# A hybrid attention block: the first batches' statistics, norm and values moved to ScalarE and GpSimd, and the end of attention in another order

## The chip, the cores and the metric

The kernel runs on one core of a Trainium2 chip. The core has TensorE (matmuls, written PE in the profile, with its weight loads as PEld), VectorE (DVE), ScalarE (ACT), GpSimd (POOL) and SyncE (SP), which issues most of the transfers. The metric is the device time of one execution in microseconds; the median over runs is compared.

## The reference

Input is `x`, 8 batches of 512 tokens with 256 channels, all in float32. Four blocks are added to it one after the other, each on the layer norm of `x`: an attention, a routed feed-forward, a gated linear attention with a SwiGLU, and the same routed feed-forward again. The change lies in the first block, except for one edit in the last.

```python
def _L0_attn_a_ref(x, Wq, bq, Wk, bk, Wv, bv, Wo, bo):      # H = 16 heads of 16 channels
    U = max(1, min(L, int(FACTOR * L)))                     # 307 of 512 queries
    q = _split_heads(x @ Wq + bq)
    k = _split_heads(x @ Wk + bk)
    v = _split_heads(x @ Wv + bv)
    scores = jnp.einsum('bhqd,bhkd->bhqk', q, k) * scale
    sparsity = scores.max(axis=-1) - scores.mean(axis=-1)
    _, top_idx = jax.lax.top_k(sparsity, U)
    ...                                                     # the chosen queries alone:
    attn = jax.nn.softmax(scores_sel, axis=-1)
    out_sel = jnp.einsum('bhuk,bhkd->bhud', attn, v)
    out = jnp.zeros_like(q).at[bi, hi, top_idx].set(out_sel)
    return out @ Wo + bo

x = x + _L0_attn_a_ref(_layernorm(x, axis=-1), ...)
x = x + _L0_ffn_ref(_layernorm(x, axis=-1), ...)
x = x + _L0_attn_b_ref(_layernorm(x, axis=-1), ...)
x = x + _L0_ffn_ref(_layernorm(x, axis=-1), ...)
```

A query that is not among the 307 of its head gives zero, so the kernel computes the attention of all queries and multiplies each result by one over its sum, or by zero.

## The kernel before

`xres` holds all of `x` in SBUF as 128 tokens x 8 batches x 4 token tiles x 256 channels. The attention works batch by batch. `front(b, pick, alone)` prepares a batch: the norm `xn` (L337 to L346), its transposes `xnT` (L357) and a centred copy `xcT` (L366 on ScalarE or L369 on VectorE), then the projections `q_ps` and `k_ps` (L384), evacuated as `qs` and `ks`, and the values `v_ps` (L423), written with their bias into `va` (L432). Queries and keys exist twice, for even and odd heads (`e`), so that four heads lie in four groups of 32 rows of TensorE.

One loop over `n` drives it. There are 128 steps of (batch, half `m`, parity `e`, token tile `k`). In each, `max_one` makes four score tiles (L487) and VectorE takes the maximum of each row into `mx` (L490). Sixteen steps later (`LAG = 16`) `exp_one` makes the transposed scores of the same heads (L498), ScalarE takes the exponential (L502), and `weigh` multiplies by the values into `av` (L507). So for the first 16 steps there are maxima alone. This is called the fill below. Here the rest of `front(0)` and all of `front(1)` are laid between the steps, piece by piece:

```python
            LAG = 16
            LEAD = 14
            ...
            first = front(0, lambda name: next(both)(name), True)
            for _ in range(6):
                next(first)
            pieces = itertools.chain(first, front(1, lambda name: next(alone)(name), True))
```

The fronts of batches 2 to 7 are laid between later steps with `alone` false. The maxima's negatives go through a transpose and small DMAs on SP into a spare row of the queries (`place_maxima`, L459) and into `neg`, one row for each batch and head.

The order of instructions on each engine is worked out by the framework, which plans with its own costs, starts from the order of the text, and keeps what depends on each other. Where the text would be planned too early, a tiny copy on GpSimd from a maximum of a given step (`maximum_of(n)`) is written into the target first, so that the instruction has to wait for it. `batch_stats` (L262) makes mean and variance of a batch on VectorE (L275, L276), the root on ScalarE (L279), its reciprocal on VectorE (L280) and a shift (L283). It is called for batch 0 ahead of the loop, for batch 1 at n = 1 (held to `xcT` of batch 0), for batch 2 at n = 5, and for batches 3 and 4 to 7 in `later_stats`, spread over the loop.

When all maxima are there, `top_queries` finds on VectorE, for the 128 rows of `work`, which queries are dropped (L536, L539). `take` (L517 to L525) copies a finished `av`, sends the rows that hold the sums of the exponentials to `den` by DMA on ScalarE's queue, and puts the rest into `outC`. `weights_of` forms `nrm` = 1/`den` where a query is chosen and 0 elsewhere (L137, L138). `weigh_outputs` spreads rows of `nrm` over channels with a small matmul (L150, a strip of 32 rows of TensorE holds two batches) and multiplies `outC` (L153). `out_unit(tail, k, b)` projects two batches' token tile `k` with `wo_a` (L163), copies on ScalarE and adds into `xres` on GpSimd. `out_projection` does the rest later with an addition on VectorE (L849, L853), and `route(0)` begins the routed feed-forward with statistics of `xres`. In the last block `down` (L955) adds the second product of a pair of batches into `xres` (L969) and sends the result out (L972).

Of the kernel before, what the change touches and what calls it, by code (L numbers as in the profile page):

```python
# [10 lines left out]
F32 = mybir.dt.float32  # L11
U8 = mybir.dt.uint8
AF = mybir.ActivationFunctionType
ALU = mybir.AluOpType
# [3 lines left out]
P = 128  # L18
# [20 lines left out]
def block_kernel(ctx: ExitStack, tc: tile.TileContext, t: dict, out: bass.AP):  # L39
# [62 lines left out]
    with ExitStack() as outer:  # L102
# [14 lines left out]

        outC = [
# [3 lines left out]
        den = a_out.tile([P, L], F32, name="den")  # L122
        neg = a_out.tile([P, L], F32, name="neg")
        mx = a_out.tile([P, NB, NC2, 2, 4 * 4], F32, name="mx")
# [5 lines left out]
        def weights_of(batches, late, late_form):  # L130


            rows = slice(16 * batches[0], 16 * batches[-1] + 16)
# [3 lines left out]
            nc.vector.reciprocal(rden[rows, :], den[rows, :])  # L137
# [5 lines left out]
        def weigh_outputs(batches):  # L143
            picks = itertools.cycle((bank, bank_m))
            for u in range(2):
                for m in range(NC2):
                    for b in batches[u::2]:
                        strip = bass.ts(b // 2, 32)
                        ps = next(picks)(f"nrm_ps{b}")
                        nc.tensor.matmul(  # L150
                            ps, spread[strip, u, m, :], nrm[strip, :], start=True, stop=True
                        )
                        nc.vector.tensor_tensor(  # L153
                            outC[b][:, m, :], outC[b][:, m, :], ps, ALU.mult
                        )
# [16 lines left out]
        with ExitStack() as inner:  # L172
# [48 lines left out]
            own = a1.tile([P, 2], F32, name="own")  # L221
            one = a1.tile([P, 2], F32, name="one")
            kept = a1.tile([P, 2], F32, name="kept")
# [34 lines left out]
            clear_values(0)  # L258

            ln = {}  # L260

            def batch_stats(batches, late=None, late_shift=None):  # L262


# [3 lines left out]
                st = a2.tile([P, n, 6], F32, tag="ln_st", name="ln_st")  # L268
                mv = a1.tile([P, n, 2], F32, tag=f"ln_mv{key}", name="ln_mv")
                rs = a1.tile([P, n], F32, tag=f"ln_rs{key}", name="ln_rs")  # L270
                sh = a1.tile([P, n], F32, tag=f"ln_sh{key}", name="ln_sh")
                for i in range(n):
                    if late is not None:
                        nc.gpsimd.tensor_copy(st[0:1, i, 0:1], late())
                    nc.vector.bn_stats(st[:, i, :], xres[:, batches[i // 4], i % 4, :])  # L275
                    nc.vector.bn_aggr(mv[:, i, :], st[:, i, :])  # L276
                    if i < n - 1:
                        yield
# [1082 lines left out]
```

## Time and profile before

| | |
|---|---|
| median of 3 runs | 1623.8 us (1623.19, 1623.8, 1629.82) |
| the profiled execution's own time | 1629.82 us |
| its span, first to last instruction | 1628.1 us |
| granted TensorE clock over the span | 0.992 |
| TensorE, VectorE, ScalarE, GpSimd busy | 98%, 60%, 42%, 21% of the span |
| the 512 maxima (L490) | 328.0 us of VectorE, 683 ns each |
| the 512 exponentials (L502) | 276.4 us of ScalarE, 597 ns each |
| first score matmul, first exponential | at 16.23 us, at 66.61 us |
| last `av` matmul ends, routed hidden matmuls begin to run together | at about 579.6 us, at 627.8 us |

A row of the profile names line, engine, operation, what is written and read, and busy time. TensorE's busy share is no measure of how full it is, since matmuls overlap and their ends are modelled. What counts for a change is the stage in which it lies and which engine is short there: the fill (up to about 66 us), the loop (to 535), the choice of queries and the last exponentials (to 580), the end of attention (to 628), and the long rest of feed-forwards and linear attention.

### The profile page before, as it was taken

What the parts mean: (1) busy time and instruction counts of PE and PEld (TensorE: products, weight loads), DVE (VectorE), ACT (ScalarE), POOL (GpSimd) and SP (SyncE); (2) the same over time, 40 slices, a digit from 0 to 9 for tenths busy, and PEclk for the clock granted to TensorE, in tenths of its full rate; (3) what the DMA queues carried; (4) which work ended last, traced back from release to release, by engine and by line L of the source; (5) the groups of instructions that cost most, each with busy time, mean ns of one, the idle gap of its engine ahead of it and who ended that gap; (6) DMA issues with size and microseconds to landing.
All of it is one profiled execution on the core that took longest, in us unless ns stands there. A gap on an engine that the chain in (4) does not pass through costs nothing.

```text
span 1628.1 us, 19814 instructions
## 1 busy us (share of the span) xinstructions
PE 1590.0 (98%) x7444; PEld 814.7 (50%) x7444; DVE 971.6 (60%) x2007; ACT 676.8 (42%) x1215; POOL 348.5 (21%) x403
## 2 busy tenths in 40 slices
PE   7999999999999999999989999999999999999999
PEld 3323323233233256655564566545655655766666
DVE  7868777676777875447753566367265633344342
ACT  3366656565655834352346124522631452121010
POOL 2111111010010043115332343145234320000000
PEclk9999999999999999999999999999999999999999
DMA  3100000000000032100000001000000010011100
GB/s 108 42 3 2 2 2 3 3 3 2 2 3 4 2 110 86 27 14 13 0 0 1 1 0 27 1 0 1 1 0 1 1 27 0 21 33 39 40 27 26
DMA packets 24951, 27.62 MB, mean 17 GB/s; under 512 B 6872, under 2 KB 21400, under 8 KB 24856
## 3 DMA queue, kind: packets, MB, share of 16 engines
q1 hardware_dynamic: 24040, 25.31, 5.4%
q8 instruction: 58, 0.95, 0.2%
q10 hardware_dynamic: 816, 1.05, 0.2%
q14 instruction: 37, 0.30, 0.1%
HBM read 21.24 MB, written 4.33 MB: 16 GB/s over the span
## 4 chain that ended last, share of the span: by engine, by line
PE 78%; DVE 12%; ACT 4%; POOL 3%; issue 2%; DMA 1%; SPq 0%; ACTq 0%; POOLq 0%; DVEq 0%
PE y_ps L964 16%; PE h_ps L984 10%; PE s L487 9%; PE s L498 9%; PE av L507 8%; PE swi_ps L1011 7%; PE proj_ps L1097 7%; DVE pr L1130 2%; DVE pr L1120 2%; PE q_ps L384 2%; PE gla_y L1222 2%; PE k_ps L384 2%; PE v_ps L423 2%; POOL o L1147 2%; DVE w L1122 1%
## 5 line engine op out<-in xcount | busy, mean ns | idle before, releaser
L490 DVE TENSOR_REDUCE mx<-s 128x1 f32<-128x512 f32 x512 | 328.0, 683 | 118.8 <-PE s L498 63.5
L502 ACT ACTIVATE e<-s 128x512 f32<-128x512 f32 x512 | 276.4, 597 | 185.2 <-PE s L498 106.8
L487 PE MATMUL s<-k,q 32*128 32x512 f32 x1024 | 301.8, 644 | 3.7 <-ACT k L414 3.2
L498 PE MATMUL s<-q,k 32*128 32x512 f32 x1024 | 297.8, 642 | 0.1
L964 PE MATMUL y_ps<-w,h 128*128 128x256 f32 x1024 | 232.5, 383 | 2.8 <-DVE h L993 2.8
L984 PE MATMUL h_ps<-xnT,w 128*128 128x512 f32 x512 | 230.1, 598 | 4.1 <-ACT h L992 4.1
L964 PEld LDWEIGHTS y_ps<-w,h 128*128 128x128 f32 x1024 | 194.0, 192 | 39.9 <-issue 10.1
L984 PEld LDWEIGHTS h_ps<-xnT,w 128*128 128x128 f32 x512 | 95.3, 191 | 112.5 <-issue 106.0
L507 PE MATMUL av<-e,va 128*32 128x512 f32 (+1 forms) x1240 | 144.4, 530 | 4.6 <-ACT e L502 3.2
L993 DVE TENSOR_TENSOR h<-h,mk 128x512 f32<-128x512 f32 x128 | 97.9, 779 | 79.7 <-ACT h L992 61.6
L487 PEld LDWEIGHTS s<-k,q 32*128 32x128 f32 x1024 | 93.9, 184 | 96.3 <-DVE mx L490 52.2
L992 ACT ACTIVATE h<-h_ps,b 128x512 f32<-128x512 f32 x96 | 65.4, 685 | 176.1 <-PE h_ps L984 176.1
L498 PEld LDWEIGHTS s<-q,k 32*128 32x128 f32 x1024 | 91.1, 183 | 75.6 <-ACT e L502 50.3
L969 DVE TENSOR_TENSOR xres<-xres,y_ps 128x512 f32<-128x512 f32 x48 | 32.8, 683 | 160.7 <-PE y_ps L964 123.5
L1011 PE MATMUL swi_ps<-zT,w_gate 128*128 128x512 f32 x256 | 122.6, 599 | 4.8 <-DVE h L1020 4.6
L1011 PE MATMUL swi_ps<-zT,w_up 128*128 128x512 f32 x256 | 121.4, 594 | 0.0
L964 PE MATMUL y_ps<-w_down,h 128*128 128x256 f32 x512 | 116.9, 380 | 0.0
L1097 PE MATMUL proj_ps<-q_w,rT 128*128 128x512 f32 x256 | 116.1, 594 | 0.3 <-ACT al L1080 0.3
L964 PEld LDWEIGHTS y_ps<-w_down,h 128*128 128x128 f32 x512 | 95.6, 190 | 19.5 <-issue 8.0
L1017 ACT ACTIVATE h<-swi_ps 128x512 f32<-128x512 f32 x64 | 38.2, 596 | 155.5 <-PE swi_ps L1011 155.3
L1147 POOL TENSOR_TENSOR o<-o,pr 128x512 f32<-128x512 f32 (+2 forms) x56 | 81.1, 1449 | 58.6 <-DVE pr L1130 56.6
L507 PEld LDWEIGHTS av<-e,va 128*32 128x32 f32 x1240 | 25.5, 108 | 123.6 <-issue 102.4
(203 smaller groups left out, 1722.1 us busy)
## 6 DMA issues: line engine op xcount, KB each, us to landing
mk<-md SPq DMA_DIRECT2D x32, 256.0 KB
out<-xres SPq DMA_DIRECT2D x16, 256.0 KB
xres<-in_L_attn_a_x SPq DMA_DIRECT2D x7, 512.0 KB
q<-negT SPq DMA_DIRECT2D x128, 2.0 KB
neg<-negT SPq DMA_DIRECT2D x128, 2.0 KB
w<-in_f_w1T SPq DMA_DIRECT2D x1, 1024.0 KB
w<-in_f_w2T SPq DMA_DIRECT2D x1, 1024.0 KB
w_gate<-in_b_w_gateT SPq DMA_DIRECT2D x1, 1024.0 KB
```

What stands on the lines that cost most here:

```text
L487: nc.tensor.matmul(s, qs[e][rows, m, bass.ts(k, P)], ks[e][rows, m, :], start=True, stop=True)
L490: nc.vector.tensor_reduce(mx[:, b, m, e, r : r + 1], s, AX.X, ALU.max)
L498: nc.tensor.matmul(s, ks[e][rows, m, bass.ts(kt, P)], qs[e][rows, m, :], start=True, stop=True)
L502: nc.scalar.activation(ex, s, AF.Exp, scale=1.0 / DH**0.5)
L507: nc.tensor.matmul(av[32 * j : 32 * j + 32, queries], va[:, 8 * kt + 4 * m + j, e, :], es[j][:, queries], start=(kt == 0), stop=(kt == 3 a ...
L964: nc.tensor.matmul(y[0][:, bass.ts(i, D)], h[f][:, bass.ts(2 * u + i, P)], w[:, f, :], start=(f == 0), stop=(f == NF - 1),)
L984: nc.tensor.matmul(ps, w1[:, c, bass.ts(f, P)], xT[g][:, c, :], start=(c == 0), stop=(c == NC2 - 1),)
L992: nc.scalar.activation(hf, ps, AF.Relu, bias=b1[:, f : f + 1])
L993: nc.vector.tensor_tensor(hf, hf, mk[g][:, f, :], ALU.mult)
L1011: nc.tensor.matmul(ps, w[:, c, bass.ts(f, P)], zT[g][:, c, :], start=(c == 0), stop=(c == NC2 - 1),)
L1097: nc.tensor.matmul(ps, rT[b // G4][:, c, bass.ts(b % G4, P)], q_w[:, c, m], start=(c == 0), stop=(c == NC2 - 1),)
L1147: nc.gpsimd.tensor_tensor(dst, dst, src, ALU.add)
```

## The change

- `early_stats` replaces `batch_stats` for batches 1 and 2. It sums `x` and the squares of `x` less its mean by accumulating activations on ScalarE, takes the root there, and leaves a reciprocal to VectorE and the shift to GpSimd. Both are held to the maximum of the step before. After batch 2's root an exponential of one column is issued.
- The norm of batches 1 and 2 is made on GpSimd as a multiply and add; batch 1's was on ScalarE, batch 2's on VectorE. The centred copy of batch 2 goes from VectorE to ScalarE.
- The values of batches 0 and 1 are copied out of PSUM by ScalarE and get their bias on GpSimd.
- The roots of batches 3 and 4 to 7 are made by three rounds of Newton's iteration on GpSimd from a first guess in integer arithmetic on VectorE.
- A batch's rows in `den`, `neg` and `nrm` are placed by `row_of`, so that neighbouring batches lie in different strips. `den` becomes two tiles, for batches 0 to 5 and 6 to 7, both filled with ones. `mx` holds four batches in turn.
- Outputs are weighed pair by pair, with output units between the pairs.
- In the last pair of the last tile each batch is added and sent out by itself.

```diff
+        def row_of(b, m, e):
+            return 32 * (b % 4) + 16 * (b // 4) + 8 * e + 4 * m
...
-        mx = a_out.tile([P, NB, NC2, 2, 4 * 4], F32, name="mx")
+        mx = a_out.tile([P, 4, NC2, 2, 4 * 4], F32, name="mx")
...
+        picks = itertools.cycle((bank, bank_m))
+        def weigh_outputs(b):
+            for m in range(NC2):
+                for c in (b, b + 1):
+                    strip = bass.ts(c % 4, 32)
+                    ps = next(picks)(f"nrm_ps{c}")
+                    nc.tensor.matmul(
+                        ps, spread[strip, c // 4, m, :], nrm[strip, :], start=True, stop=True
+                    )
+                    nc.vector.tensor_tensor(
+                        outC[c][:, m, :], outC[c][:, m, :], ps, ALU.mult
+                    )
...
+            for i in range(2):
+                nc.gpsimd.memset(den[i], 1.0)
...
+            def early_stats(b, late):
+                sm = a1.tile([P, 3, 4], F32, tag=f"ln_sm{b}", name="ln_sm")
+                sums, less, squares = (sm[:, i, :] for i in range(3))
...
+                own = a2.tile([P, L], F32, tag="e", name="ln_x", bufs=10)[:, 0:D]
+                for i in range(4):
+                    nc.gpsimd.tensor_copy(sums[0:1, i : i + 1], late)
+                    nc.scalar.activation(
+                        own, xres[:, b, i, :], AF.Identity, accum_out=sums[:, i : i + 1]
+                    )
+                nc.gpsimd.tensor_scalar(less, sums, -1.0 / D, None, ALU.mult)
+                for i in range(4):
+                    nc.scalar.activation(
+                        own, xres[:, b, i, :], AF.Square, bias=less[:, i : i + 1],
+                        accum_out=squares[:, i : i + 1],
+                    )
+                nc.scalar.activation(rs, squares, AF.Sqrt, bias=eps, scale=1.0 / D)
+                if b == 2:
+                    nc.scalar.activation(root, rs[:, 0:1], AF.Exp)
+                nc.vector.reciprocal(rs, rs)
+                nc.gpsimd.tensor_tensor(sh, less, rs, ALU.mult)
...
+            def one_by_root(rs, var, n):
...
+                nc.gpsimd.tensor_scalar(v, var, LN_EPS, None, ALU.add)
+                nc.vector.tensor_scalar(
+                    rs.bitcast(I32), v.bitcast(I32), -0.5, float(0x5F3759DF), ALU.mult, ALU.add
+                )
+                for _ in range(3):
+                    nc.gpsimd.tensor_tensor(u, v, rs, ALU.mult)
+                    nc.gpsimd.tensor_tensor(u, u, rs, ALU.mult)
+                    nc.gpsimd.tensor_scalar(u, u, -0.5, 1.5, ALU.mult, ALU.add)
+                    nc.gpsimd.tensor_tensor(rs, rs, u, ALU.mult)
...
-                    if alone and b > 0:
-                        nc.scalar.activation(
-                            xn[:, k, :], xres[:, b, k, :], AF.Identity, bias=sh, scale=rs
+                    if sh is not None:
+                        nc.gpsimd.tensor_scalar(
+                            xn[:, k, :], xres[:, b, k, :], rs, sh, ALU.mult, ALU.add
                         )
...
-                    if alone and b > 0:
+                    if b in (1, 2):
                         nc.scalar.mul(mean, xsum[:, c : c + 1], -1.0 / L)
                         nc.scalar.activation(xcT[:, c, :], ps, AF.Identity, bias=mean)
...
+                        if alone:
+                            nc.scalar.copy(home, v)
+                            nc.gpsimd.tensor_tensor(home, home, bias, ALU.add)
+                        else:
+                            nc.vector.tensor_tensor(home, v, bias, ALU.add)
...
-                    for _ in batch_stats(batches, lambda: maximum_of(n - 1)):
+                    for _ in batch_stats(batches, lambda: maximum_of(n - 1), True):
...
-            near = {
-                1: batch_stats([1], lambda: fronts[0][3][0:1, 1, 0:1], maximum_of(0)),
-                5: batch_stats([2], lambda: maximum_of(n - 1)),
-            }
...
-                    for _ in near.get(n, ()):
-                        pass
+                    if n in (1, 5):
+                        early_stats(1 + n // 5, maximum_of(n - 1))
...
-            weigh_outputs(range(NB - 2))
-            last = outC[NB - 3][0:1, 1, 0:1]
-            weights_of(range(NB - 2, NB), last, last)
+            for b in (0, 2):
+                weigh_outputs(b)
             for k in range(2):
-                for b in range(0, NB - 2, 2):
+                out_unit(tail, k, 0)
+            weigh_outputs(4)
+            last = outC[5][0:1, 1, 0:1]
+            weights_of(slice(P // 2, P), 1, last, last)
+            for b in (2, 4):
+                for k in range(2):
                     out_unit(tail, k, b)
-            weigh_outputs(range(NB - 2, NB))
+            weigh_outputs(6)
...
-            if i == 1 and half == 1:
+            if last and k == 3 and b == NB - 2:
+                if half == 1:
+                    x = xres[:, b + i, k, :]
+                    nc.vector.tensor_tensor(x, x, y[0][:, bass.ts(i, D)], ALU.add)
+                    nc.sync.dma_start(out=out_v[:, b + i, k, :], in_=x)
+            elif i == 1 and half == 1:
                 nc.vector.tensor_tensor(tokens(k, b), tokens(k, b), pairs(y[0]), ALU.add)
```

## The prediction

> **What bounds the kernel now.** I read the page's busy shares first, then the windows, then the chain of waits and the timeline of the stages that the diff touches.
>
> ```profile
> PE 1590.0 (98%) x7444; PEld 814.7 (50%) x7444; DVE 971.6 (60%) x2007; ACT 676.8 (42%) x1215; POOL 348.5 (21%) x403
> ```
>
> TensorE fills the span, so VectorE's 60% says little by itself. The windows show that the first stage is of another kind (columns: stretch, length, then PE, PEld, DVE, ACT, POOL busy, granted clock, DMA share, GB/s):
>
> ```profile
> 20.00:40.00 20.00, 19.93 (x87) 9.19 (x85) 18.80 (x42) 6.45 (x14) 4.91 (x12) 0.99 0.24 76
> 40.00:60.00 20.00, 19.56 (x81) 7.90 (x80) 19.10 (x37) 5.93 (x9) 7.49 (x6) 1.00 0.20 61
> ...
> 200.00:240.00 40.00, 40.00 (x254) 12.14 (x251) 29.80 (x52) 23.95 (x48) 5.17 (x4) 1.00 0.01 2
> ```
>
> From 20 to 60 us VectorE is busy 37.9 of 40 us and ScalarE 12.4, GpSimd 12.4. From 200 on VectorE has a quarter to spare and TensorE none. So work taken off VectorE pays only in the fill, the first 16 steps, which make maxima and no exponentials. The chain of waits says what starts the fill and what paces it (start, us, what):
>
> ```profile
> 7.38 5.96 DMA xres<-in_L_attn_a_x
> ...
> 14.96 0.23 DVE ln_mv L276 x2
> 15.19 0.03 issue
> 15.22 0.03 ACT ln_rs L279
> 15.24 0.18 issue
> 15.42 0.77 ACT k L414
> 16.19 0.04 issue
> 16.23 1.43 PE s L487 x8
> ...
> 53.02 4.86 DVE mx L490 x8
> 57.87 0.66 DVE va L432 x2
> 58.54 2.42 DVE mx L490 x4
> 60.96 0.66 DVE va L432 x2
> 61.62 2.39 DVE mx L490 x4
> ```
>
> The first score matmul waits for k, and k stands on ScalarE behind a root that waits for the statistics of batch 1, whose data land at 13.3. Later the chain is maxima (4 in 2.4 us) with values between them. In the loop one wait of TensorE touches the change (total us, times, longest), beside one row of ScalarE's timeline:
>
> ```profile
> PE av L507 <- ACT e L502: 3.2, 2, 1.8
> ```
>
> ```profile
> 108.85 1.28 ACT L279 ACT_TABLE_LOAD   x1
> ```
>
> **The change part by part.** *Start.* Batch 1's statistics leave the front of the queues: they now wait for the first maximum. The projection for k ends at 13.0 (timeline: `k_ps` at 11.14 for 1.89), its first evacuation takes 0.77, so scores start at 13.8, not 16.23: minus 2.4 us. ScalarE pays later: 8 passes of 128x256 at 0.52 (four `xn` in 2.08) plus 0.19 for each accumulator read, a root of 0.30 and two hand-overs to GpSimd of some 0.3 are 6.6 us. This runs from about 16 to 23 and delays batch 0's second query evacuation (22.84 before) by little. Then GpSimd normalizes: four at 0.615 (row L1229, 128x256) are 2.5 us, done by 26 to 28. The transposes that need it stood at 34.4, and at 29 to 30 with the other gains. TensorE's queue is in order, so a later `xn` would stop the score matmuls behind it; there are about 2 us to spare. GpSimd's own queue holds the clearing of `va` (1.8) behind it, which batch 1's values need only after 50.
>
> *Fill.* What leaves VectorE after 17.6: eight value additions, 3.0 us; batch 2's statistics, four pairs at a pitch of 0.34 plus 0.09, 1.7; its `xn`, 1.3; its shift, 0.1; its first centred copy with the mean, 0.9. Together 7.0, less 0.2 for the reciprocal of batch 1 that now falls here: 6.8. ScalarE gains 6.6 for batch 2 (in its gap between 27.3 and 35.6), eight value copies at about 0.4, 3.2, and 1.8 for the centred copies (0.69 and 0.20 twice); it loses `xn`, 2.1. Its 26 us before 66 become 42, still under the 50 or so there. GpSimd gains five normalizations' worth, 2 x 2.5, and eight additions at 0.77 (row L1089) to 0.90 (L1161), 6 to 7: its 18 become 30. No DMA is moved past another on SP; only the loads' triggers come earlier with the maxima.
>
> Here a rule speaks against the change. The GpSimd row for 128x256 is 0.615 and VectorE's is 0.394; the Trainium skill, "GPSIMD Engine Reference", section 4.1 Engine selection, says that ordinary elementwise work belongs on VectorE, GpSimd being about twice as slow with two inputs, and section 1 that its SBUF interface is shared with VectorE. By the rule the moved work costs more and might slow VectorE too. The trace has a test: from 51.5 to 58.5 GpSimd adds without pause, and eight maxima take 4.88, 0.61 each, as in 61.54 with GpSimd idle (2.47 for four). So I charge no contention; by the rule 64 maxima slowed by a tenth would take 4 us back.
>
> Without the 6.8 VectorE needs 64 x 0.61 = 39.0 plus 1.7 of small work. TensorE needs as much: 16 x 1.07 for scores, 7.9 for the rest of batch 0's front (four projections at 1.0, values 3.9), 13.1 for batch 1's, 1.2 of transposes: 39.3. Two engines that hand over through seven banks will not both run full, so I take 5.5 of the 6.8 (bounds 2 and 6.8).
>
> *Entry to the loop.* Batch 2's second centred copy, 0.9, leaves VectorE, and the exponential's table is loaded early: before, the load stood from 65.32 to 66.60 with the first scores ready. Against this ScalarE makes the two centred copies amid its first exponentials. Minus 1.5 (bounds plus 1 and minus 3).
>
> *Loop.* The roots of batch 3 and of batches 4 to 7 take no table. The trace shows two switches there and back, 1.28 per load with nothing after it, 5.1 us of ScalarE; TensorE lost 1.4 and 1.8. The Trainium skill, "ScalarE: Activation LUTs", section What ACT_TABLE_LOAD costs, puts a switch at 2.66 with its drain: 10.6, and TensorE would gain 8. The activation at 110.14 follows the load of 108.85 at once, so the trace decides: minus 3.2. Newton's 13 GpSimd operations, at 0.19 each by the smallest rows, are 2.5 us twice on an engine 13% busy; VectorE's one is 0.2. What waits behind them is `outC`, used at 580. I take minus 3.0.
>
> *End of attention.* Rows are laid out so that neighbours b and b+1 have different strips, and outputs 0 to 5 are weighed pair by pair. Before, twelve products (0.62 each from 581.47) stood in an order by which output units started at 585.85 and ran from 587.65; pair 0 is now ready after four, 583.95. The units then fill TensorE while the other products run: minus 2 at the first unit. Later 8 units at 1.78 (9.33 for 42 matmuls) and three weighing groups end near 600, where out_projection started at 605.94. The second reciprocal (3.35) comes no earlier than before, and it feeds batches 6 and 7: their products can't end before 598. Between 0 and minus 6 I take minus 4. The fill of `den` with ones is two memsets of a quarter of `va`'s 1.80 each, before 7 us, when GpSimd waits for weights anyway.
>
> *Last tile.* The last addition is 0.4 instead of 0.69 and the last transfer half as large; but the first addition reads half of a bank whose other half TensorE is about to write, which the trace shows nowhere. If that serializes, TensorE stands for 0.5. Bounds minus 0.7 and plus 0.6; I take 0.
>
> The sum is 2.4 + 5.5 + 1.5 + 3.0 + 4.0 = 16.4. The profiled execution took 1629.8 (span 1628.1), so it would be 1613.4. That execution is 6 us above the median and holds stretches at half clock (68 to 75 us at 0.50), of which I count nothing as gained. From the median, 1623.8, the forecast is 1607.4.
>
> **Rivals.**
> *TensorE takes over the fill.* Its 39.3 is as long as VectorE's new total, its queue is in order, and 7 steps from 44.5 to 62.0 already ran at 2.5 us. If the pace stays near 2.9 instead of 3.1 per step, the fill yields 3; with 1.5 at the end of attention and the start and loop as above the sum is 9.9: 1614. For it: score loads wait both for maxima and for issue. Against it: TensorE waits on VectorE in half of the early steps.
>
> *ScalarE becomes late in the fill.* Its queue carries statistics, values and centred copies between the evacuations that free banks. If every evacuation is late by 0.5, 16 of them take 8 back; the start and the loop remain, in part: 4 us, 1620. Against it: gaps of 6 to 8 us stand in its row before.
>
> *The loop's rhythm breaks: slower.* The engines' orders are planned anew. Between 80 and 530 us I read 204 half-steps whose eight score records stand together: 152 took 1.1 us, 26 took 1.3, 14 took 1.4, where banks came free in pairs. Each break costs 0.25 with no other engine to absorb it. `mx` now has four batches, so maxima also wait for transposes, and starts shift. With 100 more broken half-steps, 25 us, all is lost and 8 more: 1632. It decides against the change from 66 on. Against it: those transposes are 64 steps old, and nothing of the loop's bank use is edited.
>
> **How the numbers follow.** A measurement of this kernel can tell about 0.5%, 8 us, from no change: faster means below 1615.7. The forecast has a chance of 0.62, with its own range of 1601 to 1614. TensorE in the fill has 0.20, of which three parts in four lie below 1615.7. ScalarE late has 0.10, and the broken rhythm 0.08, most of it slower. That makes faster 0.77, same 0.16, slower 0.07. The range of 1600 to 1620 leaves out the slow case, half of the ScalarE case and a twentieth below.
>
> **What would show it.** Right: first scores near 13.8; VectorE between 15 and 56 nearly all maxima at 0.61; the first exponential scores near 56 instead of 64.5; no table load between 70 and 580 and no 1.4 us stop of `av`; the first output unit some 2 us after the first weighing, and the first routed hidden matmuls 16 us earlier. Wrong: transposes of batch 1 waiting for `xn`, scores waiting for ScalarE's value copies, more half-steps of 1.3 us, or the gain at 80 us gone by 540.

## The result, and the profile after

| | us | runs |
|---|---|---|
| before, on the same chip | 1627.4 | 6, from 1623.2 to 1629.9 |
| after | 1637.3 | 6, from 1634.3 to 1639.1 |
| ratio | 1.0063, 95% interval 1.0043 to 1.0082 | |

The changed kernel is slower, by 0.6%. The forecast was 1607.4. The kernel before was timed again in five later sets of 14 to 44 runs, with medians of 1627.7 to 1629.1, so the 1623.8 from which the forecast was set out was low by about 4.

The profiled execution of the changed kernel took 1634.33 us (span 1632.5). Its first row, the busy shares, says little:

```profile
PE 1584.1 (97%) x7444; PEld 810.5 (50%) x7444; DVE 958.7 (59%) x1971; ACT 681.8 (42%) x1250; POOL 366.1 (22%) x450
```

VectorE has lost 13 us of work, ScalarE and GpSimd have gained 5 and 18, all as intended. The windows say where the time went (columns: stretch, length, then PE, PEld, DVE, ACT, POOL busy, granted clock, DMA share, GB/s):

```profile
20.00:40.00 20.00, 16.70 (x71) 7.08 (x70) 12.30 (x24) 11.59 (x34) 8.74 (x20) 0.91 0.18 57
40.00:60.00 20.00, 17.96 (x70) 6.49 (x71) 16.15 (x30) 9.33 (x19) 8.73 (x11) 0.91 0.23 61
...
100.00:120.00 20.00, 13.97 (x81) 4.64 (x82) 9.81 (x20) 8.59 (x16) 7.04 (x17) 0.86 0.01 3
...
200.00:220.00 20.00, 16.09 (x97) 4.79 (x94) 11.85 (x23) 7.74 (x15) 4.82 (x10) 0.83 0.00 1
```

From 20 to 60 VectorE is busy 28.5 of 40 us instead of 37.9, but TensorE too has lost: 34.7 instead of 39.5, and its clock is down. An engine that was relieved and then stands idle was not the only bound, or now waits for something. And in two stretches of the loop, where TensorE had nothing to spare, it stands for 6.0 and 3.9 us. TensorE's list of waits (engine, line, releaser: total us, times, longest) gives them names:

```profile
PE s L539 <- DVE mx L542: 11.4, 4, 6.0
PE xnT_ps L405 <- DVE xn L392: 6.7, 2, 6.5
PE swi_ps L1069 <- DVE h L1078: 5.1, 7, 1.4
PE q_ps L432 <- ACT xcT L414: 4.3, 1, 4.3
```

The second is at the very start and the third in the SwiGLU of the third block, and the kernel before has both. The first and the fourth are new. What `mx` waits for is in VectorE's timeline (start, us, engine, line, operation, and in brackets the idle time before it and what ended that):

```profile
109.29 0.17 DVE L303 TENSOR_SCALAR ln_rs<-ln_v 128x4 int32<-128x4 int32 x1 [0.36 <-POOL ln_v L302]
109.37 0.68 DVE L542 TENSOR_REDUCE mx<-s 128x1 f32<-128x512 f32 x1
114.61 1.38 DVE L392 TENSOR_SCALAR xn<-xres,ln_mv,ln_rs 128x256 f32<-128x256 f32 x4 [4.56 <-POOL ln_rs L310]
115.91 1.28 DVE L542 TENSOR_REDUCE mx<-s 128x1 f32<-128x512 f32 x2
```

Batch 3's norm `xn` stands at the head of VectorE's queue and needs Newton's last product from GpSimd. For 4.56 us VectorE does nothing, though maxima behind `xn` are ready to be taken; the four banks of score matmuls fill, and TensorE stops. GpSimd's timeline in the same time:

```profile
109.55 0.20 POOL L307 TENSOR_TENSOR ln_u<-ln_v,ln_rs 128x4 f32<-128x4 f32 x1 [0.29 <-DVE ln_rs L303]
...
110.68 0.20 POOL L307 TENSOR_TENSOR ln_u<-ln_v,ln_rs 128x4 f32<-128x4 f32 x1
110.86 0.77 POOL L576 TENSOR_SCALAR st<-st,marks 128x512 f32<-128x512 f32 x1
...
111.74 1.27 POOL L577 TENSOR_TENSOR outC<-outC,st 128x512 f32<-128x512 f32 x1
...
114.37 0.20 POOL L310 TENSOR_TENSOR ln_rs<-ln_rs,ln_u 128x4 f32<-128x4 f32 x1
```

Each of the small operations lasts 0.20 but the next starts 0.28 later, and two pieces of `outC` work, 2.0 us, stand between them. From 109.02 to 114.57 the chain takes 5.6 us. After the stop TensorE's granted clock is 0.50 until about 121.

Four stretches, cut by marks that every kernel has, make the rest comparable: up to the first weighed sum (`av`), from there to the first reciprocal of the weights, to the first routed hidden matmul, and to the last one. The last stretch holds the same code in all kernels.

| profile of | first `av` at | loop | end of attention | the rest |
|---|---|---|---|---|
| before | 74.6 | 500.9 | 47.7 | 986.7 |
| before, a second profile | 73.8 | 500.8 | 47.7 | 981.7 |
| after | 74.0 | 511.6 | 46.5 | 982.0 |

The loss is the loop's 10.7 us. The last column varies by itself, between 981.7 and 987.1 in the 20 profiles of this study, so differences of a few us in one profile's span prove nothing.

### The profile page after: what moved, and what is told of

The parts are those of the page before. It is cut to its first block, busy times and chain, and to the rows that moved or that the text cites. A ratio compares the mean times of both kernels' runs of the same rounds, so it can differ in the third digit from the quotient of the medians.

```text
span 1632.5 us, 19879 instructions
## 1 busy us (share of the span) xinstructions
PE 1584.1 (97%) x7444; PEld 810.5 (50%) x7444; DVE 958.7 (59%) x1971; ACT 681.8 (42%) x1250; POOL 366.1 (22%) x450
## 4 chain that ended last, share of the span: by engine, by line
PE 78%; DVE 11%; ACT 5%; POOL 3%; issue 2%; DMA 1%; SPq 0%; POOLq 0%; ACTq 0%; DVEq 0%
PE y_ps L1016 16%; PE h_ps L1042 10%; PE s L539 9%; PE s L550 9%; PE av L559 8%; PE swi_ps L1069 7%; PE proj_ps L1155 7%; DVE pr L1188 2%; DVE pr L1178 2%; PE q_ps L432 2%; PE k_ps L432 2%; PE v_ps L471 2%; PE gla_y L1280 2%; POOL o L1205 2%; DVE w L1180 1%
## 5 line engine op out<-in xcount | busy, mean ns | idle before, releaser
L539 PE MATMUL s<-k,q 32*128 32x512 f32 x1024 | 302.6, 652 | 12.4 <-DVE mx L542 11.4
L1155 PE MATMUL proj_ps<-q_w,rT 128*128 128x512 f32 x256 | 116.1, 594 | 0.3 <-ACT al L1138 0.3
L924 POOL TENSOR_TENSOR xres<-xres,b 128x512 f32<-128x512 f32 x32 | 40.1, 1272 | 207.8 <-ACT row L863 185.4
```

The lines of the kernel that those rows point to most:

```text
L539: nc.tensor.matmul(s, qs[e][rows, m, bass.ts(k, P)], ks[e][rows, m, :], start=True, stop=True)
L1155: nc.tensor.matmul(ps, rT[b // G4][:, c, bass.ts(b % G4, P)], q_w[:, c, m], start=(c == 0), stop=(c == NC2 - 1),)
```

## The experiments

Each kernel was timed beside the kernel before on the same chip (1627.7 to 1629.1 in these sets).

**1. Is it Newton?** The first of four kernels has only `newton=False` for the later statistics:

```diff
-                    for _ in batch_stats(batches, lambda: maximum_of(n - 1), True):
+                    for _ in batch_stats(batches, lambda: maximum_of(n - 1), False):
```

> The changed kernel with one thing undone: the roots of batch 3 and of batches 4 to 7 are made by ScalarE's Sqrt and VectorE's reciprocal again; everything else is kept. Theory (Newton's chain on GpSimd stops VectorE's in-order queue, and through the maxima TensorE, which then runs at half clock): TensorE's stops of 6.0 us at 110 and of some 4 us at 205 go, the two table loads there and back (4 x 1.28 us on ScalarE, some 3 us of TensorE) return; 1637 minus some 9, near 1628, and the first reciprocal of the weights back from 585.5 to about 577. Rival (the loop lost its time by its new order and the ring of four maxima batches, and the stop at 110 only shows it in one place): within 3 us of the changed kernel, 1634 to 1640, and the first reciprocal of the weights stays near 585.

Measured: 1624.0 (ratio to before 0.9977, interval 0.9968 to 0.9986), so 13 us better than the change and better than before. The loop is 501.8, and TensorE's waits for `mx` fall from 11.4 to 1.1 us. The rival is out: with the same ring of maxima, and an order planned anew as well, TensorE is busy 475.3 of the 480 us from 80 to 560, as it was before (475.3). The loop gives 9.8 of the 13 us; the rest is not placed, since the profiled execution of the change is the fastest of its six and that of this kernel the slowest of its twelve.

The second is the kernel before with `one_by_root` added to it and used for batches 3 to 7:

```diff
-                nc.scalar.activation(rs, mv[:, :, 1], AF.Sqrt, bias=eps)
-                nc.vector.reciprocal(rs, rs)
+                if newton:
+                    one_by_root(rs, mv[:, :, 1], n)
+                else:
+                    nc.scalar.activation(rs, mv[:, :, 1], AF.Sqrt, bias=eps)
+                    nc.vector.reciprocal(rs, rs)
```

> The kernel before with one part of the change alone: Newton's iteration on GpSimd for the roots of batch 3 and of batches 4 to 7, as the change writes it. Theory: VectorE waits for 13 dependent GpSimd operations at a pitch of 0.28 to 0.4 us twice, TensorE stops twice for 4 to 6 us and runs at half clock after it; 1627 plus 7 to 10, 1634 to 1637. Rival (the loop's order, not Newton): no loss or a gain of up to 3 us, 1624 to 1628.

Measured: 1636.0 (1.0049, 1.0033 to 1.0065). The loop is 511.2, 10 us longer than before. The one part brings nearly the whole loss with it: 8.3 by the medians here, 13.3 on top of the rest of the change. The loops don't differ by that, but this profile reaches its first `av` at 71.0 instead of 74.6 (experiment 5 comes back to it).

The third moves the 13 operations to VectorE:

```diff
-                    nc.gpsimd.tensor_tensor(u, v, rs, ALU.mult)
+                    nc.vector.tensor_tensor(u, v, rs, ALU.mult)
```

> The changed kernel with Newton's 13 operations moved from GpSimd to VectorE, the same arithmetic. Theory: what costs is the length of the chain while VectorE's queue stands behind it; on VectorE 14 tiny operations at 0.06 to 0.18 us are 1 to 2.5 us, so TensorE stops for 1 to 2 us instead of 6 and 4 and no table is loaded: some 1626, faster than the Sqrt version by 0 to 3. Rival (order of the loop): within 3 us of the changed kernel, 1634 to 1640. Should the Sqrt version be fast and this one slow, then the arithmetic's own length matters and not the engine.

Measured: 1633.0 (1.0036, 1.0025 to 1.0046). I expected 1626. The stop of TensorE falls only from 6.0 to 4.4 us. VectorE's timeline shows why:

```profile
110.64 0.65 DVE L303 TENSOR_SCALAR ln_rs<-ln_v 128x4 int32<-128x4 int32 x1
111.19 0.68 DVE L542 TENSOR_REDUCE mx<-s 128x1 f32<-128x512 f32 x1
111.79 0.84 DVE L307 TENSOR_TENSOR ln_u<-ln_v,ln_rs 128x4 f32<-128x4 f32 x1
112.66 0.16 DVE L308 TENSOR_TENSOR ln_u<-ln_u,ln_rs 128x4 f32<-128x4 f32 x1
...
114.65 0.16 DVE L310 TENSOR_TENSOR ln_rs<-ln_rs,ln_u 128x4 f32<-128x4 f32 x1
114.85 1.06 DVE L392 TENSOR_SCALAR xn<-xres,ln_mv,ln_rs 128x256 f32<-128x256 f32 x3
```

Two of the tiny operations take 0.65 and 0.84 instead of 0.17 and 0.16, the others start every 0.20, and `xn` follows at 114.85: the maxima are held up for 3 us of arithmetic and 1 us of norm. GpSimd's timeline has the reason for the two long ones:

```profile
110.49 0.77 POOL L576 TENSOR_SCALAR st<-st,marks 128x512 f32<-128x512 f32 x1 [0.77 <-DMA den<-st]
111.34 1.27 POOL L577 TENSOR_TENSOR outC<-outC,st 128x512 f32<-128x512 f32 x1
```

They end when GpSimd's operations end: 111.29 beside 111.26, 112.63 beside 112.61. The maximum between them, which reads PSUM, has its usual 0.68. The Trainium skill, "SBUF — State Buffer", section "SBUF: two separate sides", says that GpSimd shares a pair of SBUF ports with those VectorE operations that read two SBUF inputs or run in a two-port mode, under an exclusive lock held for a whole instruction. The second row agrees with it, since that operation reads two SBUF inputs; in which mode the first one ran, no row shows.

The fourth undoes the early statistics: `batch_stats` for batches 1 and 2 at their old places, batch 1's norm on ScalarE, batch 2's on VectorE, no early exponential.

```diff
-                    if n in (1, 5):
-                        early_stats(1 + n // 5, maximum_of(n - 1))
+                    for _ in near.get(n, ()):
+                        pass
```

> The changed kernel with the statistics and norms of batches 1 and 2 as they were before (VectorE's bn_stats, ScalarE's root, the norm of batch 1 on ScalarE and of batch 2 on VectorE, no early load of the exponential's table); values on ScalarE and GpSimd, Newton and the end of attention stay. Theory (VectorE's reciprocals stood in its queue 2.64 and 2.81 us for ScalarE's late roots, and gave back most of what left VectorE): the fill ends within 1.5 us of where it does in the changed kernel, so 1635.5 to 1640. Rival A (the early statistics do pay, the values on ScalarE and GpSimd are what slows the fill): slower than the changed kernel by 3 to 6, 1640 to 1643. Rival B (they are a pure loss): faster by 3 or more, below 1634.

Measured: 1634.3 (1.0033, 1.0020 to 1.0045), 3 us better than the change and at the edge of rival B. The fill gains even more, the first `av` comes at 69.5 instead of 74.0, but the loop with its two Newton stops took 514.6 in this profile. So what was to relieve VectorE made the fill longer.

**2. Is it Newton, or what stands behind it?** The next kernel keeps Newton on GpSimd and only lets VectorE meet the norm later:

```diff
+                if b in (3, 4):
+                    for k in range(4):
+                        nc.gpsimd.tensor_copy(xn[0:1, k, 0:1], maximum_of(n - 1))
                 for k in range(4):
                     mean, rs, sh = ln[b, k]
```

> The changed kernel with Newton's iteration on GpSimd as it is, but VectorE's norms of batches 3 and 4 held back: a tiny GpSimd copy of the newest maximum into each of their four tiles makes them stand in VectorE's queue behind the maxima of step 29 and of step 45, when the chain is over. Theory (it is not Newton that costs, but the norm that stands behind it at the head of VectorE's in-order queue): both stops of TensorE go, no table is loaded, 1624 (the version with Sqrt) minus some 3, so 1620 to 1623, and TensorE's waits for maxima fall from 11.4 us to under 2. Rival (the chain disturbs the loop by itself, through GpSimd's outputs or by a new order, as its 1633 on VectorE might also say): 1630 or more.

Measured: 1624.1 (0.9976, 0.9965 to 0.9987), just above what was expected. Four one-element copies per batch bring back 13 us. In VectorE's timeline of this kernel the maxima go on through the whole chain, which runs from 110.6 to 116.1 here:

```profile
110.84 0.17 DVE L303 TENSOR_SCALAR ln_rs<-ln_v 128x4 int32<-128x4 int32 x1 [0.36 <-POOL ln_v L302]
110.92 1.88 DVE L545 TENSOR_REDUCE mx<-s 128x1 f32<-128x512 f32 x3
113.42 1.29 DVE L545 TENSOR_REDUCE mx<-s 128x1 f32<-128x512 f32 x2 [0.61 <-PE s L553]
115.08 0.76 DVE L495 TENSOR_TENSOR va<-v_ps,bv 128x256 f32<-128x256 f32 x2 [0.38 <-PE v_ps L474]
116.17 1.29 DVE L545 TENSOR_REDUCE mx<-s 128x1 f32<-128x512 f32 x2 [0.34 <-PE s L542]
```

The loop takes 498.1, against 500.6 to 501.8 of every kernel with table loads: the 3 us that the absent loads were to give are there. TensorE's waits say so too: two waits for `e`, 3.2 us together in the version with Sqrt, are gone, and those for `mx` are 1.5 us. In the median the gain doesn't show beside the version with Sqrt, and why is open; this profile has a rest of 987.1, the longest of all.

Beside it ran three kernels with Sqrt. The first also undoes the early statistics:

> Two parts undone: the early statistics of batches 1 and 2 and Newton; values on ScalarE and GpSimd, the end of attention and the last tile stay. Theory: the two losses add, 1637.3 minus 13.3 minus 3.0 = 1621, and the first weighed sum starts at 69.5 instead of 75.3. Rival (the gain of undoing the early statistics was seen only beside the Newton stops, as a shifted meeting of queues): as the version with Sqrt alone, 1623 to 1625.

Measured: 1620.6 (0.9953, 0.9937 to 0.9970). The two losses add. The first `av` comes at 71.8, though, not at the 69.5 that was expected.

The second also gives the values of batches 0 and 1 back to VectorE:

```diff
-                        if alone:
+                        if False:
                             nc.scalar.copy(home, v)
```

> Of the change only the order at the end of attention (with its rows, the two tiles of sums and the ring of maxima), the last tile and the joined marks are left; statistics, norms, values and roots are as before. Theory: the end of attention gains 1.6 to 3 us (first output unit 3.1 us after the first weighing instead of 5.5), the last tile nothing: 1627.7 minus 1.5 to 3, 1624.5 to 1626. So the values on ScalarE and GpSimd are worth the rest, some 4 us, to the kernel with both parts undone. Rival (all that is gained is at the end, the values give nothing): within 1 us of that kernel, 1620 to 1622.

Measured: 1622.7 (0.9967, 0.9957 to 0.9978), 5.7 better than before, twice what I expected. One thing of the change was left in it that the expectation does not name: the mean and centred copy `xcT` of batch 2 stayed on ScalarE (`b in (1, 2)`). Experiment 5 takes this up. The values are worth 2.1 by the medians, and the intervals overlap.

The third takes the early root apart from its reciprocal:

```diff
-                nc.scalar.activation(rs, squares, AF.Sqrt, bias=eps, scale=1.0 / D)
+                nc.scalar.activation(squares, squares, AF.Sqrt, bias=eps, scale=1.0 / D)
...
-                nc.vector.reciprocal(rs, rs)
+                nc.vector.reciprocal(rs, squares)
```

> The version with Sqrt for batches 3 to 7, and in the early statistics the root written in place over the squares, so that VectorE's reciprocal no longer has to wait for the early exponential that reads the root, nor for its table load of 1.28. Theory: VectorE's stand at the reciprocal of batch 2 falls from 2.8 to 3.0 us to about 1.3, the fill ends 1 to 1.5 us earlier, 1622.5 to 1623.5. Rival (the copy xcT, late in ScalarE's queue, sets TensorE's stop of 4.3 us at 42, and the reciprocal is hidden by it or the other way round): within 0.5 us of the version with Sqrt, 1624.

Measured: 1625.0 (0.9983, 0.9975 to 0.9991). No gain: VectorE's stand at batch 2 went from 2.95 to 2.63 only, since the root itself is that late.

**3. What stops TensorE in the fill?** My theory was that VectorE's stands at the two early reciprocals, 2.64 and 2.81 us, give back what it was spared. So they were held behind later maxima:

```diff
+                def close(late):
+                    nc.gpsimd.tensor_copy(rs[0:1, 0:1], late)
+                    nc.vector.reciprocal(rs, squares)
...
+                    if n in (3, 8):
+                        close(maximum_of(n))
```

> The version with Sqrt for batches 3 to 7 and with the root over the squares, and the two early reciprocals held back by a tiny GpSimd copy of a maximum (batch 1's behind the maximum of step 3, batch 2's behind that of step 8), so that VectorE meets them when the roots are done. Theory (VectorE's stands of 2.6 us each at these reciprocals are what the early statistics lose): no stand of VectorE before them, the fill ends 2 to 4 us earlier than with Sqrt alone (first weighed sum near 72 instead of 75), 1620 to 1622 instead of 1624. Rival (ScalarE's queue, late with xcT and the queries, is what stops TensorE in the fill; the stands only fall together with it): no change, 1623.5 to 1625.5, and TensorE's wait for xcT stays or turns up at another of ScalarE's tiles.

Measured: 1624.8 (0.9975, 0.9966 to 0.9984), first `av` at 75.2. The first stand is down to 0.27 and the second is gone, yet nothing is gained; the theory fell. TensorE's timeline of this kernel names the other cause:

```profile
36.46 0.66 PE L410 MATMUL xnT_ps<-ident,xn 128*128 128x128 f32 x4
42.10 2.08 PE L437 MATMUL q_ps<-xnT,wq 128*128 128x512 f32 x2 [4.98 <-ACT xcT L419]
```

Batch 1's transposes end at 37.1 and their copies are wanted at once, but ScalarE's timeline has this:

```profile
38.16 0.30 ACT L288 ACTIVATE ln_sm<-ln_sm,eps 128x4 f32<-128x4 f32 x1
38.47 1.28 ACT L291 ACT_TABLE_LOAD   x1
...
39.87 0.63 ACT L494 COPY va<-v_ps 128x256 f32<-128x256 f32 x2
40.39 0.61 ACT L413 ACTIVATE xnT<-xnT_ps 128x512 f32<-128x512 f32 x1
...
41.36 0.69 ACT L419 ACTIVATE xcT<-xnT_ps,xmean 128x512 f32<-128x512 f32 x1
```

Batch 2's eight passes run from 32.96 to 38.1, then root and table load; batch 1's evacuations stand behind them in the same queue. The two matmuls after the stop take 2.08 instead of 1.13: half clock. So in the next set batch 2's statistics were made at step 9, behind those evacuations (norms held, root over the squares), once without and once with held reciprocals:

```diff
-                    if n in (1, 5):
-                        early_stats(1 + n // 5, maximum_of(n - 1))
+                    if n in (1, 9):
+                        early_stats(1 + n // 9, maximum_of(n - 1))
```

> The changed kernel with the norms of batches 3 and 4 held (as the run at 1624.1), the root over the squares, and batch 2's early statistics made at step 9 instead of step 5, so that batch 1's transposed copies and xcT stand ahead of them and of the early table load in ScalarE's queue. Theory (that queue stopped TensorE for 4 to 5 us at 42): the stop goes or falls under 2, the first weighed sum starts near 71 instead of 75.5, 1619 to 1621. Rival (the 5 us of statistics and the table load only move, and stop the evacuations of batch 1's q and k, and TensorE for their banks, somewhat later): 1623 to 1625, with a new wait of TensorE between 44 and 56.

Measured: 1620.8 (0.9959, 0.9945 to 0.9973).

> As the one with batch 2's statistics at step 9, and both early reciprocals held behind later maxima (of steps 3 and 12). Theory: with ScalarE's queue out of the way VectorE's two stands of 2.6 us now show, so another 1 to 3 us less than without the holds: 1617 to 1619. Rival (the stands lie beside TensorE's other work): within 1 us of it.

Measured: 1617.8 (0.9944, 0.9927 to 0.9961), first `av` at 70.4. TensorE's timeline of the latter:

```profile
34.81 0.66 PE L413 MATMUL xnT_ps<-ident,xn 128*128 128x128 f32 x4
35.65 1.13 PE L440 MATMUL q_ps<-xnT,wq 128*128 128x512 f32 x2 [0.18 <-ACT xcT L422]
...
47.18 1.13 PE L547 MATMUL s<-k,q 32*128 32x512 f32 x4 [1.74 <-ACT k L470]
```

The stop of 5 us is gone. The rival is a little right: 1.74 us turn up at 47, where the statistics now stand before an evacuation of `k`. And the reciprocals do matter once ScalarE is out of the way: 3 us by the medians, with intervals that overlap, and 2.5 by the first `av` (72.9 and 70.4).

**4. What is the best version?** Without early statistics and with held norms:

> The early statistics undone, Newton on GpSimd kept but with VectorE's norms of batches 3 and 4 held behind later maxima; values, end of attention and last tile as changed. Theory: the best of both, no stop in the loop and no table load there, and the fill of the version with early statistics undone: 1620.5 minus 0 to 3, so 1617.5 to 1620.5. Rival (the two table loads there and back are worth nothing, as the 1624.1 of the held version beside the 1624.0 of the Sqrt version suggests): 1620 to 1621.5.

Measured: 1618.3 (0.9943, 0.9927 to 0.9958), loop 498.1, first `av` at 69.4. The same with the last tile in one piece, and with the values on VectorE:

> The version with the early statistics undone and held norms (1618.3), and the last tile in one piece as before. Theory: 0 to 0.8 less, as beside the Sqrt version (1619.8 against 1620.6): 1617.5 to 1618.3. Rival (that was chance): 1618.3 to 1619.

Measured: 1617.5 (0.9939, 0.9922 to 0.9956).

> The version with the early statistics undone and held norms (1618.3), and the values of batches 0 and 1 by VectorE again. Theory: eight additions of 0.37 us return to VectorE, which is busy nine tenths of the fill: 1 to 3 us more, 1619.3 to 1621.3, as the kernels with Sqrt (1622.65 against 1620.55). Rival (TensorE has as much to do in the fill and hides them): within 0.7 us of 1618.3.

Measured: 1618.5 (0.9941, 0.9925 to 0.9956). The rival holds here: values on ScalarE and GpSimd are worth 0.2, not measurable. Beside the Sqrt version the last tile was tried too:

> The version with the early statistics and Newton undone, and the last tile's addition and transfer in one piece again as before. The prediction put the last tile at 0; the trace of the changed kernel has TensorE stand 0.58 us for the first addition and a tail of 3.2 instead of 3.7 us after the last addition's start. Theory: no measurable difference to the version with the split last tile, 1620.5 plus or minus 0.7. Rival (the split costs what TensorE stands): 0.5 to 1 us faster than it.

Measured: 1619.8 (0.9950, 0.9935 to 0.9966). Twice undoing it gave 0.8, each time within the intervals. The version at 1617.5 beats both kernels: by 20 us the changed one, by 11 the one before. Early statistics, even in their best place (1617.8), are no better than none (1618.3).

**5. What else did the kernel with the end alone gain?** A second profile of the kernel before, and two more kernels:

> The kernel before, unchanged, for a second profile of it: whether TensorE's half clock between 68 and 75 us belongs to it. If it does, the first weighed sum starts again at 74 to 75 and part of what the kernel with the end of attention alone gained (it started at 70.3) is a clock that it kept by not stopping there; if not, it starts at 71 and the span is some 3 us shorter than the 1628.1 of the first profile.

One execution, 1623.9, first `av` at 73.8. The half clock is there again, in windows of 2 us:

```profile
66.00:68.00 2.00, 2.00 (x9) 0.74 (x8) 2.00 (x6) 1.01 (x3) 0.00 (x0) 0.81 0.00 0
68.00:70.00 2.00, 2.00 (x5) 0.49 (x6) 1.63 (x4) 0.63 (x2) 0.00 (x0) 0.50 0.00 0
70.00:72.00 2.00, 2.00 (x6) 0.49 (x10) 0.55 (x1) 0.49 (x1) 0.00 (x0) 0.50 0.00 0
```

The next kernel is the one before with one line of the change, then the end alone with that line undone:

```diff
-                    if alone and b > 0:
+                    if b in (1, 2):
                         nc.scalar.mul(mean, xsum[:, c : c + 1], -1.0 / L)
                         nc.scalar.activation(xcT[:, c, :], ps, AF.Identity, bias=mean)
```

> The kernel before with one thing of the change: the mean and the centred copy xcT of batch 2 by ScalarE instead of VectorE (0.89 us twice between the first maxima beside exponentials). Theory (this is what spares the half clock at 67 to 74 us): the first weighed sum starts at 70 to 71 instead of 73.8 to 74.6, 1625 to 1626 instead of 1628. Rival (chance of the order, or something at the start): within 1 us of the kernel before, the half clock stays.

Measured: 1626.2 (0.9990, 0.9981 to 0.9999), first `av` at 70.9, and the windows keep their clock:

```profile
66.00:68.00 2.00, 2.00 (x11) 0.93 (x8) 2.00 (x6) 1.99 (x3) 0.00 (x0) 1.00 0.04 8
68.00:70.00 2.00, 2.00 (x8) 0.48 (x11) 1.06 (x2) 1.25 (x3) 0.00 (x0) 1.00 0.00 0
```

> The kernel with the end of attention alone, now with batch 2's centred copies by VectorE too as before. Theory: only the 3 us at the end of attention remain (from the first reciprocal to the routed hidden matmuls 44.6 instead of 47.7): 1625 to 1626, and the half clock at 67 to 74 is back. Rival (the order alone makes both): 1622 to 1623.

Measured: 1624.4 (0.9980, 0.9971 to 0.9989), first `av` at 73.3 with the half clock back, end of attention 44.5. Moving the two centred copies off VectorE goes with 3 us in the profile and 1.6 in the median; the end is worth 3.

That the copies set off the half clock is not shown by this pair, since it also comes and goes without them. Of the four profiles with the copies on VectorE, the kernel before with Newton alone kept a clock of 1.00 there (first `av` at 71.0). Of the 16 with the copies on ScalarE, one ran at 0.50 from 68 to 74: the version with Sqrt and the last tile in one piece (first `av` at 72.7), whose code is the same as that of the 1620.6 version up to the last tile. So the half clock is rarer with the copies on ScalarE, 1 of 16 against 3 of 4, and that is all that these profiles show.

## Why the prediction was wrong

The kernels form a chain in which one part is added at a time. Medians, each minus the one before it (sets on different chips, in which the kernel before differed by 1.7 at most):

| step | median | difference | predicted |
|---|---|---|---|
| before | 1627.8 | | |
| + end of attention, with last tile | 1624.4 | -3.4 | -4 and 0 |
| + centred copies of batch 2 on ScalarE | 1622.7 | -1.7 | part of the -1.5 at the entry and of the -5.5 of the fill |
| + values on ScalarE and GpSimd | 1620.6 | -2.1 | in the -5.5 of the fill |
| + early statistics, norm on GpSimd | 1624.0 | +3.5 | the rest of the -5.5, and -2.4 at the start |
| + Newton on GpSimd | 1637.3 | +13.3 | -3.0 |

- *Loop*, minus 3.0: this is the step that decided. Its saving was sized right: with the norms held the loop is 498.1 to 498.3 us long instead of 500.6 to 501.8. What failed is "Newton's 13 GpSimd operations, at 0.19 each by the smallest rows, are 2.5 us twice on an engine 13% busy", and after it "What waits behind them is `outC`, used at 580". The durations were right (0.20) but the pitch in a dependent chain is 0.28, and `outC` work stood between: 5.6 us. Above all I asked what was queued behind the chain on GpSimd and not who waited for its result: VectorE's `xn`, which the planner had put right behind, and behind that the maxima on which TensorE lives. The stops were 6.0 and some 4 us, and half clock followed. A term with plus 13 was booked as minus 3.
- *Fill*, minus 5.5 with bounds of 2 and 6.8: out of its bounds, plus 1.4 with the values. VectorE is busy 9.4 us less between 20 and 60, but 4.4 of these are maxima that had not run by then (45 instead of 52), so some 5 are what left it. Two steps failed. "0.2 for the reciprocal" counted its duration and not that VectorE stands before it, 2.64 and 2.81 us. And ScalarE's "42, still under the 50 or so there" summed its work over the stage (and too high: the windows to 66 us show 21.2 before and 30.2 after); what counted was the order: batch 2's statistics and the table load, 7 us, ahead of batch 1's `xnT` and `xcT`. The second is the one that set the time; the first showed only when the second was gone. "I charge no contention" rested on maxima, which read PSUM, and held for them. It does not hold for VectorE's work on SBUF: in the version with Sqrt batch 3's four norms took 2.15 instead of 1.38 while GpSimd worked on `outC`.
- *Start*, minus 2.4: not there. The first score matmul started at 15.03 instead of 16.23, but over all profiles it lies between 14.1 and 16.1 with early statistics and between 14.3 and 16.2 without, so the term is lost in what that start varies by itself. The step that failed is the wait of `k` for the root, which I took from one execution: in the first profile of before `k` started 2.4 us after its projection, in the second 0.4.
- *Entry*, minus 1.5: near in size (1.7), by luck. The early table load was not needed for it: the kernel with the end and the centred copies alone has none and enters the loop at 70.3. What was gained in that profile is the half clock at 67 to 74, of which I had said "I count nothing as gained"; it comes less often with the centred copies on ScalarE.
- *End of attention*, minus 4: near, but in part for another reason. The order came true: the first units started 3.1 us after the first weighing, not 2, before 5.5:

```profile
590.37 3.03 PE L156 MATMUL nrm_ps<-nrm,spread 32*128 32x512 f32 x16 [0.74 <-DVE nrm L143]
593.46 3.72 PE L169 MATMUL ao_ps<-wo_a,outC 128*128 128x256 f32 x16
597.11 1.99 PE L156 MATMUL nrm_ps<-nrm,spread 32*128 32x512 f32 x8
599.03 7.17 PE L169 MATMUL ao_ps<-wo_a,outC 128*128 128x256 f32 x32
```

  The stretch is 3.1 us shorter (44.5 or 44.6 instead of 47.7) in 13 of the 16 profiles with the new order. Some 1.7 of this is clock. All four profiles with the old order have a piece at half clock in the stretch, in three of them at the last 16 matmuls of the units, as here in the second profile of before:

```profile
599.57 5.41 PE L163 MATMUL ao_ps<-wo_a,outC 128*128 128x256 f32 x16
```

  In the kernel at 1617.8 the same 16 run at full clock:

```profile
592.33 3.72 PE L169 MATMUL ao_ps<-wo_a,outC 128*128 128x256 f32 x16
```

  The changed kernel's own profile has that half clock too, and its stretch is 46.5, only 1.2 shorter than before. So the order itself gives 1.2 to 1.5, and the rest is that the half clock came in 3 of 16 profiles instead of 4 of 4. Why it is rarer stays open.

- *Last tile*, 0: right within the noise, and the stand of 0.5 that was feared is there, 0.58 in the changed kernel's timeline, against a tail shorter by 0.5 (3.2 us from the last addition to the end, 3.7 before):

```profile
1625.54 3.72 PE L1016 MATMUL y_ps<-w,h 128*128 128x256 f32 x16 [0.58 <-DVE xres L1024]
```

Of the rivals, *ScalarE becomes late in the fill* named the right place but charged it to late bank evacuations of half a microsecond each; it was one stop of 4 to 5. *The loop's rhythm breaks* gave 1632, the nearest number, by a mechanism that did not happen. The true one, a short operation that waits at the head of VectorE's queue, was priced nowhere. The baseline adds 4 us: of the three runs of before two were at its lower edge.

## What to carry to other kernels

When a small computation is moved to an idle engine, follow its result and not its work: find the first instruction that waits for it, on which in-order queue that stands, and what is queued behind. If that queue feeds the engine that bounds the kernel, a chain of 13 tiny operations costs its whole length and the clock after it, and holding the consumer back behind work that is ready (here a one-element copy from a later maximum) turned the loop's 511.6 us into 498.1, the gain that was meant. A sum of busy times in a stage shows room on an engine, but not that its queue has the urgent work in front.

## What the hardware did that I had not expected

- Dependent GpSimd operations on 128x4 last 0.20 us and start every 0.28; on VectorE they last 0.16 and start every 0.20. Sixteen columns instead of four change this to 0.22 and 0.30 on GpSimd.
- A VectorE operation on SBUF of 0.16 us took 0.84 beside a GpSimd addition of 1.27 and ended with it; a maximum from PSUM beside the same additions kept its 0.68.
- After stops of 6.0 and 3.9 us in the loop TensorE ran at a clock of 0.50 for 4 to 6 us more, and after the stop of 6.0 in the kernel with the early statistics undone for 9. But the half clock of the kernel before at 67 to 74 us came in both its profiles with TensorE shown busy in every window from 66 on. What in the rows sets it off there stays open.
- The 980 us after attention, the same code in all kernels, took between 981.7 and 987.1 us from profile to profile. A gain of 3 us elsewhere can be hidden in a single run by this alone.
